# A gated cross-attention kernel: the second x load ahead of the setup's last store, both bias DMAs at later slots

## The chip, the cores and the metric

The kernel runs on one core of one Trainium2 chip. The metric is the device time of one execution in microseconds (us); the median of several runs is compared. PE is the engine for matmuls, DVE the vector engine, ACT the engine for activations and copies, POOL the general-purpose engine, SP the engine that only issues DMAs. Each engine runs its own instructions strictly in the order of the program; engines wait for each other through semaphores.

## The reference

Everything is float32. `x` is 8 x 1024 x 1024, the context (memory) 8 x 64 x 512.

```
memory_proj = einsum('bme,de->bmd', memory, W_mem)
scores  = einsum('bnd,bmd->bnm', x, memory_proj) / sqrt(1024)
attn    = softmax(scores)
context = einsum('bnm,bmd->bnd', attn, memory_proj)
gate    = sigmoid(concat([x, context]) @ W_gate.T + b_gate)
fused   = x + gate * context
out     = fused * rsqrt(mean(fused**2) + 1e-6) * norm_w
```

## The kernel before

The tokens are worked in 16 "quads" of 512 tokens, numbered from 0. The product of a quad's x with the upper half of `W_gate` is done by a fast matrix scheme with seven outer products, visited in the order 1, 6, 7, 5, 4, 2, 3; each outer product is again seven inner products (`af`, `kB`, `kC`, `ed`, `ed`, `af`, `af`), each one "slot" of the plan, so that a quad has 49 slots. For outer product o of quad q there is a set of left sums `l` (tile `l2_q_o`, four instructions on POOL, made while the outer product before it runs), two PSUM banks `af` and `ed`, and two single banks `b` (for `kB`) and `c` (for `kC`). DVE empties `kB` and `kC` into `u`, so the next outer product's `kB` on PE waits until DVE has read the last one. POOL (`pre`) adds the sums `u3` (512 wide) and `u4` (256 wide) into the tiles `gate_0` to `gate_3`, and DVE (`fin_ed`, `fin_af`) adds the banks `ed` and `af` on top; so one outer product's additions wait for POOL's, and POOL's for DVE's `u`. Below, `u_6`, `l_5`, `kB_5` and so on carry the number of the outer product.

Beside this run the attention's scores and softmax. The context's part of the gate is not computed from the context: a matrix `mg`, memory times the lower half of `W_gate`, is made once in the setup, stored to DRAM (`mgd`), and loaded for each batch element: 64 rows for each of two halves. A matmul of the attention with `mg` ("visit", `pc<-mg,attnT` and `af<-mg,attnT`) adds the gate's context part. The first visits of a quad stand in outer product 4 and use the banks `b` and `c` that its `kB` and `kC` have just used; the second stand in outer product 3.

The bias `b_gate` is added to `mg` once: a DMA that accumulates, issued by POOL, adds it to the 64 loaded rows of the first batch element in SBUF (`add_bias` on `mgs[0][M:P]`), a second, larger one (448 rows) to the rows of the other seven in DRAM (`mgd[1, M:]`). These are the first two DMAs that POOL issues; later it issues `residual`, four each quad, which add x to the gated result.

A quad's x is loaded by four DMAs of 512 KB on SP's queue (`load_xq`) into one tile `xq`; the pool has one buffer, so a load waits until the eight transposes of the quad before (DVE, `a<-xq`) have read it. The setup ends with four stores of `mg` (c11, c22, c21, c12 in this order) and `load_mg`, which waits for them.

What runs when is set by two means: the setup is written out by hand, and the main part by the table `plan(q)`, whose `at(slot, ...)` puts a call at a slot. Within an engine the program's order is kept. Slot 0 begins with the `af` matmul at 78.72 us of the profiled execution.

Of the kernel before, what the change touches and what calls it, by code (L numbers as in the profile page):

```python
# [15 lines left out]
P = 128  # L16
# [4 lines left out]
def tile_gated_cross_attention_rmsnorm(  # L21
# [44 lines left out]
    M, E = mem.shape[1:]  # L66
# [10 lines left out]
    Q4 = D // 4  # L77
# [4 lines left out]
    xqpool = ctx.enter_context(tc.tile_pool(name="xqpool", bufs=1))  # L82
# [12 lines left out]
    def tt(eng, o, a, b, op):  # L95
        pin(eng.tensor_tensor(o, a, b, op))  # L96

    def load(o, i):
        pin(nc.sync.dma_start(o, i))

    def t4k(pool, shape, tag, name):
        return pool.tile(shape, F32, tag=tag, name=name)
# [5 lines left out]
    def chunks(t, n):  # L108

        return t.rearrange("p s e -> p (s e)").rearrange("p (m j) -> p j m", j=n)  # L110
# [34 lines left out]
    load(nw_sb, norm_w.partition_broadcast(P))  # L145
    xq = {}

    def load_xq(q, i):
        b, n0 = q // QPB, (q % QPB) * QT
        if i == 0:  # L150
            xq[q] = t4k(xqpool, [P, 16, Q4], "xq", f"xq{q}")
        src = x[b, n0 : n0 + QT, :].rearrange("(s c) (i e) -> i c s e", c=32, i=4)
        load(xq[q][32 * i : 32 * (i + 1), :, :], src[i])

    R11, R21, R12, R22, T4, T1, T2 = range(7)
    outer_b = {
# [26 lines left out]
    mgd = dram.tile([2, BM, D], F32, name="mgd")  # L183
# [168 lines left out]
    sTs, attnTs, scs, mxs, dens, mps, mgs = {}, {}, {}, {}, {}, {}, {}  # L352
# [3 lines left out]
    def transpose_x(q, t, half):  # L356

        key = q, t // 2, half
        if key not in A:
            A[key] = t4k(  # L360
                apool, [P, KH, 2 * P], f"a{t // 2 + 1}{half + 1}", f"a{t // 2 + 1}{half + 1}_{q}"
            )
        r = t % 2
        pin(
            nc.vector.transpose(  # L365
                A[key][:, :, r * P : (r + 1) * P],
                chunks(xq[q][:, 4 * t : 4 * t + 4, :], KD)[:, half * KH : (half + 1) * KH],
            )
        )

    def outer_s(q, n):
        a11, a12, a21, a22 = (A.get((q, r, h)) for r in range(2) for h in range(2))
        if n == 3:
            S[q, 3] = a21
            tt(nc.vector, a21, a11, a21, ALU.subtract)
            return
        s = S[q, n] = t4k(apool, [P, KH, 2 * P], f"s{n}", f"s{n}_{q}")
        if n == 1:
            tt(nc.vector, s, a21, a22, ALU.add)
        elif n == 2:  # L380
            tt(nc.vector, s, S[q, 1], a11, ALU.subtract)
        else:
            tt(nc.vector, s, a12, S[q, 2], ALU.subtract)
# [153 lines left out]
    def store_mpT(r, h):  # L537
        load(mpd[:, h * KH : (h + 1) * KH, r * HM : (r + 1) * HM], mpT[r][h])
# [90 lines left out]
    def mg_tile(pool, tag, name):  # L629
        return t4k(pool, [P, 2, H], tag, name)  # L630
# [10 lines left out]

    s1 = mp_step(nc.vector, "s1", apool, m21, m22, ALU.add)
    store_mpT(0, 1)
    for i in range(4):
        load_xq(0, i)
    c11 = mg_tile(rot, "u", "mg_c11")
    c12 = mg_tile(rot, "u", "mg_c12")
    c21 = mg_tile(rot, "l2", "mg_c21")
# [49 lines left out]
    store_mg(c21, 1, 0)  # L698
    for t in (2, 3):
        transpose_x(0, t, 1)  # L700
    outer_s(0, 1)
    for n in range(2):
        inner_sum(nc.vector, 4, n)
# [10 lines left out]
    def at(slot, fn, *args):  # L714
        due.setdefault(slot, []).append(lambda: fn(*args))

    def mid(key, fn, *args):
        beside.setdefault(key, []).append(lambda: fn(*args))
# [5 lines left out]
    def plan(q):  # L724
        t0 = SLOTS * q
        nxt = q + 1 < NQ
        if q == 0:
            at(t0 + 7, scores, q)
            at(t0 + 8, add_scores, q)
        at(t0 + (3 if q else 8), outer_s, q, 3)  # L730
        for i, o in enumerate(ORDER):
            for part, t in ((0, 1), (1, 2)):
                if i + 1 < len(ORDER):
                    at(t0 + 7 * i + t, inner_s, q, ORDER[i + 1], part)
                elif nxt:
                    at(t0 + 7 * i + t, inner_s, q + 1, ORDER[0], part)
        at(t0 + (11 if q else 18), outer_s, q, 4)
        when = (9, 10, 11, 15, 16, 19, 23) if q == 0 else (1, 8, 9, 13, 15, 19, 23)
        steps = (
            turn_scores,  # L740
            softmax_max,
            softmax_exp,
            softmax_sum,
            softmax_scale,
            turn_attn,
            attn_difference,
        )
        for t, fn in zip(when, steps):
            at(t0 + t, fn, q)
        if not nxt:  # L750
            at(t0 + 12, load_last)
            return
        for i in range(4):
            at(t0 + 2 + (0 if q else 4 * i), load_xq, q + 1, i)
        for i, t, half in (
            (20, 0, 0), (21, 1, 0), (23, 2, 0), (25, 3, 0), (37, 2, 1), (38, 3, 1), (42, 0, 1)
        ):
            at(t0 + i, transpose_x, q + 1, t, half)
        mid((q, 3, 1), transpose_x, q + 1, 1, 1)
        mid((q, 3), scores, q + 1)  # L760
        at(t0 + 46, add_scores, q + 1)
        mid((q, 3), outer_s, q + 1, 1)
        mid((q, 3), outer_s, q + 1, 2)
        if (q + 1) % QPB == 0:
            at(t0 + 10, load_mp, (q + 1) // QPB)
            at(t0 + 29, turn_mp, (q + 1) // QPB)
            at(t0 + 31, store_mp, (q + 1) // QPB)
            at(t0 + 49, load_mg, (q + 1) // QPB)
        if q == 0:
            at(t0 + 10, add_bias, mgs[0][M:P, :])  # L770
            at(t0 + 20, add_bias, mgd[1, M:, :])

    for o in (2, 3):
        w1_place(o)
# [389 lines left out]
    for q in range(NQ):  # L1164
        plan(q)
        for o in ORDER:
            outer_product(q, o)
# [29 lines left out]
```

## Time and profile before

| what | us |
|---|---|
| median of 3 runs (lowest, highest) | 947.88 (947.78, 948.89) |
| the profiled execution's own time | 947.87 |
| its span, first to last instruction | 946.1 |
| PE busy in the span | 932.3 |
| DVE, POOL, ACT busy | 801.0, 738.8, 432.6 |
| quad 0's x issued by SP from | 32.69 |
| last store of `mg` issued | 79.53 |
| `mg` loads issued from | 80.12 |
| quad 1's x issued from | 83.06 |
| first bias DMA on POOL | 97.44 |
| second bias DMA on POOL | 106.23 |

The time of an execution is the span and 1.8 us around it. A PE that is busy for 932.3 of 946.1 us leaves little; whatever can be won or lost is in the places where PE waits. The waits are read in the view of waits by engine, then followed in the chain of waits (each step is what released the next) and in the timelines of single engines.

### The profile page before, as it was taken

Reading aid. Unit: us, or ns where it says so; the run is one execution under the profiler, and the core shown is the slowest. Engines: PE = TensorE matmul, PEld = TensorE weight load, DVE = VectorE, ACT = ScalarE, POOL = GpSimd, SP = SyncE. Lnnn points to the kernel's source line nnn. Section 1 sums busy time; section 2 is a strip of 40 time slices with the busy share of each in tenths; the row PEclk is TensorE's granted clock in tenths of the full one; section 3 lists DMA queues with packets and bytes.
Section 4 is the critical chain, followed back from the end, with each engine's and each line's share of the span. In section 5 each row is a group of like instructions: output and inputs, shape, how many; then the busy total and the mean of one; then the engine's idle time right before and its main releaser. Section 6 shows DMA issues by size and latency. Waiting matters only on the chain.

```text
span 946.1 us, 15921 instructions
## 1 busy us (share of the span) xinstructions
PE 932.3 (99%) x5572; PEld 727.5 (77%) x5572; DVE 801.0 (85%) x1267; ACT 432.6 (46%) x1111; POOL 738.8 (78%) x814
## 2 busy tenths in 40 slices
PE   9999899999999999999999999999999999999995
PEld 8646678687877778687777778787777778787774
DVE  6798788888897889888897889888897889888887
ACT  4212327263643627264543627264543617264556
POOL 5998878778696868778696868878696868868695
PEclk9999999999999999999999999999999999999998
DMA  9926565491918366491918466491918466390632
GB/s 378 309 69 149 87 113 131 106 197 36 219 58 173 95 142 138 101 200 33 216 65 168 100 136 143 96 206 28 220 65 163 106 130 150 87 205 34 135 154 90
DMA packets 71184, 128.44 MB, mean 136 GB/s; under 512 B 12608, under 2 KB 49472, under 8 KB 70848
## 3 DMA queue, kind: packets, MB, share of 16 engines
q1 hardware_dynamic: 61920, 93.86, 38.0%
q0 software_dynamic: 9184, 33.56, 19.6%
q8 instruction: 45, 0.74, 0.3%
q14 instruction: 35, 0.29, 0.1%
HBM read 87.56 MB, written 41.68 MB: 137 GB/s over the span
## 4 chain that ended last, share of the span: by engine, by line
PE 93%; DVE 2%; POOL 2%; issue 1%; DMA 1%; ACT 0%; SPq 0%; POOLq 0%; DVEq 0%; ACTq 0%
PE af L93 31%; PE ed L93 20%; PE kB L93 10%; PE pc L93 10%; PE kC L93 10%; PE psT_af L93 5%; PE pm_ctx L93 3%; PE pm_af L93 2%; PE pm_ed L93 2%; POOL gate L96 1%; DVE gate L96 1%; POOL l L96 1%; DMA wm<-in_w_mem_t 1%; PE psT_ed L93 0%; DVE u L96 0%
## 5 line engine op out<-in xcount | busy, mean ns | idle before, releaser
L96 POOL TENSOR_TENSOR gate<-gate,u 128x512 f32<-128x512 f32 (+1 forms) x224 | 245.5, 1108 | 151.7 <-DVE u L96 150.8
L795 ACT ACTIVATE gate<-gate 128x512 f32<-128x512 f32 x127 | 80.0, 631 | 182.4 <-DVE gate L96 180.8
L365 DVE STREAM_TRANSPOSE a<-xq 128x512 f32<-128x512 f32 x128 | 141.8, 1111 | 9.0 <-PE af L93 8.0
L96 POOL TENSOR_TENSOR l<-a 128x256 f32<-128x256 f32 x128 | 110.0, 859 | 17.4 <-PE af L93 15.8
L93 PE MATMUL pc<-mg,attnT 64*64 64x512 f32 x512 | 117.0, 596 | 0.1
L93 PE MATMUL kB<-it,l 128*128 128x256 f32 x448 | 115.0, 379 | 1.3 <-POOL l L96 1.3
L93 PE MATMUL ed<-it,l 128*128 128x256 f32 x448 | 115.0, 379 | 0.0
L824 DVE SCALAR_TENSOR_TENSOR gate<-gate,ss,nw_sb 128x512 f32<-128x512 f32 x120 | 110.2, 918 | 1.1
L93 PE MATMUL af<-w,a 128*128 128x256 f32 x384 | 98.5, 379 | 0.0
L1049 ACT COPY u<-af 128x256 f32<-128x256 f32 x112 | 41.5, 371 | 122.8 <-PE af L93 112.7
L96 DVE TENSOR_TENSOR gate<-gate,pc 128x512 f32<-128x512 f32 x128 | 85.5, 677 | 11.9 <-ACT gate L795 11.9
L93 PEld LDWEIGHTS kB<-it,l 128*128 128x128 f32 x448 | 85.0, 190 | 13.2 <-POOL l L96 1.6
L93 PEld LDWEIGHTS ed<-it,l 128*128 128x128 f32 x448 | 85.1, 190 | 11.6
L96 DVE TENSOR_TENSOR gate<-gate,ed 128x512 f32<-128x512 f32 x112 | 76.4, 682 | 17.3 <-POOL gate L96 15.4
L96 DVE TENSOR_TENSOR gate<-gate,af 128x512 f32<-128x512 f32 (+1 forms) x128 | 76.1, 605 | 16.3 <-PE af L93 10.5
L96 POOL TENSOR_TENSOR l<-s 128x256 f32<-128x256 f32 x96 | 84.7, 882 | 1.2 <-issue 1.2
L93 PEld LDWEIGHTS af<-w,a 128*128 128x128 f32 x384 | 73.0, 190 | 10.3 <-issue 0.5
L93 PEld LDWEIGHTS pc<-mg,attnT 64*64 64x64 f32 x512 | 32.8, 132 | 49.8 <-issue 23.3
L93 PE MATMUL ed<-it,a 128*128 128x256 f32 x256 | 67.4, 386 | 0.0
L93 PE MATMUL af<-mg,attnT 64*64 64x512 f32 (+1 forms) x380 | 67.0, 457 | 0.0
L96 DVE TENSOR_TENSOR u<-u,kB 128x256 f32<-128x256 f32 x112 | 46.0, 411 | 24.7 <-PE kB L93 23.7
L93 PE MATMUL af<-t,s 128*128 128x256 f32 x256 | 65.8, 379 | 0.0
(213 smaller groups left out, 2130.9 us busy)
## 6 DMA issues: line engine op xcount, KB each, us to landing
xq<-in_x SPq DMA_DIRECT2D x64, 512.0 KB, 10.3
gate<-in_x POOLq DMA_DIRECT2D x60, 512.0 KB, 8.3
out<-gate SPq DMA_DIRECT2D x60, 512.0 KB, 3.1
w<-in_w_gate_t SPq DMA_DIRECT2D x8, 512.0 KB, 10.2
w<-in_w_gate_t SPq DMA_DIRECT2D x2, 2048.0 KB, 16.9
mg<-mgd SPq DMA_DIRECT2D x16, 256.0 KB, 4.8
wm<-in_w_mem_t SPq DMA_DIRECT2D x4, 512.0 KB, 5.9
mpd<-mpT SPq DMA_DIRECT2D x4, 512.0 KB, 9.6
```

What stands on the lines that cost most here:

```text
L93: pin(nc.tensor.matmul(o, lhsT, rhs, start=start, stop=stop, skip_group_check=True))
L96: pin(eng.tensor_tensor(o, a, b, op))
L365: nc.vector.transpose(A[key][:, :, r * P : (r + 1) * P], chunks(xq[q][:, 4 * t : 4 * t + 4, :], KD)[:, half * KH : (half + 1) * KH],)
L795: pin(nc.scalar.activation(g, g, AF.Sigmoid))
L824: nc.vector.scalar_tensor_tensor(g[:, cols], g[:, cols], rstd[:, t % 2 : t % 2 + 1], nw_sb[:, cols], ALU.mult, ALU.mult,)
L1049: pin(nc.scalar.copy(p1, af[:, 0]))
```

## The change

Quad 1's x is no longer loaded from the table in slots 2, 6, 10 and 14, but in the setup, behind the last transpose of quad 0's x and in front of the store of c12. The first bias DMA moves from slot 10 to slot 18, the second from slot 20 to slot 24. `load_xq` issues its four parts in one call; for the other quads nothing else changes. No instruction is added or removed.

```diff
-    def load_xq(q, i):
+    def load_xq(q):
         b, n0 = q // QPB, (q % QPB) * QT
-        if i == 0:
-            xq[q] = t4k(xqpool, [P, 16, Q4], "xq", f"xq{q}")
+        xq[q] = t4k(xqpool, [P, 16, Q4], "xq", f"xq{q}")
         src = x[b, n0 : n0 + QT, :].rearrange("(s c) (i e) -> i c s e", c=32, i=4)
-        load(xq[q][32 * i : 32 * (i + 1), :, :], src[i])
+        for i in range(4):
+            load(xq[q][32 * i : 32 * (i + 1), :, :], src[i])
...
     for t in (2, 3):
         transpose_x(0, t, 1)
+    load_xq(1)
     outer_s(0, 1)
...
-        for i in range(4):
-            at(t0 + 2 + (0 if q else 4 * i), load_xq, q + 1, i)
+        if q:
+            at(t0 + 2, load_xq, q + 1)
...
         if q == 0:
-            at(t0 + 10, add_bias, mgs[0][M:P, :])
-            at(t0 + 20, add_bias, mgd[1, M:, :])
+            at(t0 + 18, add_bias, mgs[0][M:P, :])
+            at(t0 + 24, add_bias, mgd[1, M:, :])
```

PE, DVE and ACT keep their order, instruction for instruction. Two queues change.

On SP, at the end of the setup, the piece of the difference (`mg_c` are the four parts of `mg`, `mg_c_302` is c12; `xq_444` and `xq_481` are quad 1's x, `xq_928` quad 2's):

```order
 L99 DMA mgd<-mg_c_304 128x2x512
 L99 DMA mgd<-mg_c_303 128x2x512
+L99 DMA xq_444<-in_x 32x16x256 x4
 L99 DMA mgd<-mg_c_302 128x2x512
-L99 DMA mg_461<-mgd 64x1024 x2
-L99 DMA xq_481<-in_x 32x16x256 x4
+L99 DMA mg_466<-mgd 64x1024 x2
 L99 DMA xq_928<-in_x 32x16x256 x4
```

The four loads of x now stand ahead of one store and of both loads of `mg`, where they stood behind all three.

On POOL, in outer products 6 to 5 of quad 0, before (the name of a tile is followed by the outer product or, for `gate`, by the token tile):

```order
L96 TENSOR_TENSOR gate_1_496<-gate_1_496,u_6_510 128x512
L530 DMA mg_461<-in_b_gate 64x1024
L96 TENSOR_TENSOR gate_0_505<-gate_0_505,u_6_510 128x256
L96 TENSOR_TENSOR l_0_5_613<-s_0_444 128x256
L96 TENSOR_TENSOR l_0_5_613<-l_0_5_613,s_0_444 128x256
L96 TENSOR_TENSOR l_0_5_613<-s_0_444 128x256
L96 TENSOR_TENSOR l_0_5_613<-s_0_444,l_0_5_613 128x256
L96 TENSOR_TENSOR gate_3_636<-gate_1_496,u_7_606 128x512
L96 TENSOR_TENSOR gate_2_645<-gate_0_505,u_7_606 128x256
L530 DMA mgd<-in_b_gate 448x1024
L96 TENSOR_TENSOR l_0_4_668<-a_0_441 128x256
```

and the same stretch now:

```order
L96 TENSOR_TENSOR gate_1_499<-gate_1_499,u_6_512 128x512
L96 TENSOR_TENSOR gate_0_507<-gate_0_507,u_6_512 128x256
L96 TENSOR_TENSOR l_0_5_612<-s_0_449 128x256
L96 TENSOR_TENSOR l_0_5_612<-l_0_5_612,s_0_449 128x256
L96 TENSOR_TENSOR l_0_5_612<-s_0_449 128x256
L96 TENSOR_TENSOR l_0_5_612<-s_0_449,l_0_5_612 128x256
L96 TENSOR_TENSOR gate_3_635<-gate_1_499,u_7_606 128x512
L530 DMA mg_466<-in_b_gate 64x1024
L96 TENSOR_TENSOR gate_2_645<-gate_0_507,u_7_606 128x256
L96 TENSOR_TENSOR l_0_4_667<-a_0_441 128x256
```

The first bias DMA stood between the two additions of `u_6`; now it stands between the two additions of `u_7`, six instructions later. The second is gone from in front of `l_4`. It comes back a little later on POOL, between the additions of `u_5`:

```order
L96 TENSOR_TENSOR attnT_648<-attnT_648 64x256 x2
L96 TENSOR_TENSOR gate_3_635<-gate_3_635,u_5_662 128x512
L96 TENSOR_TENSOR gate_1_499<-gate_1_499,u_5_662 128x512
L530 DMA mgd<-in_b_gate 448x1024
L96 TENSOR_TENSOR gate_2_645<-gate_2_645,u_5_662 128x256
L96 TENSOR_TENSOR gate_0_507<-gate_0_507,u_5_662 128x256
```

Before, the same rows followed each other without the DMA.

More of the change, by code (lines that the diff above doesn't have):

```diff
@@ L643, in tile_gated_cross_attention_rmsnorm @@
     store_mpT(0, 1)
-    for i in range(4):
-        load_xq(0, i)
+    load_xq(0)
     c11 = mg_tile(rot, "u", "mg_c11")
@@ L752, in plan @@
             return
-        for i in range(4):
-            at(t0 + 2 + (0 if q else 4 * i), load_xq, q + 1, i)
+        if q:
+            at(t0 + 2, load_xq, q + 1)
         for i, t, half in (
```

## The prediction

> **What bounds the kernel now.** I read the page's first block, then the waits of PE, then the chain of waits around the two waits found there, then the timelines of PE, ACT, POOL and DVE between 94 and 130 us.
>
> ```profile
> PE 932.3 (99%) x5572; PEld 727.5 (77%) x5572; DVE 801.0 (85%) x1267; ACT 432.6 (46%) x1111; POOL 738.8 (78%) x814
> ```
>
> The waits of PE from 85 to 230 us (total, times, longest):
>
> ```profile
> PE af L93 <- ACT u L1049: 1.3, 1, 1.3
> PE kB L93 <- POOL l L96: 1.3, 1, 1.3
> ```
>
> PE is the bound nearly everywhere; these two waits, both in quad 0, are all the time that the change could win there. PE's timeline (start, length, what, idle before) has the places, and the pair of rows on which the argument will end:
>
> ```profile
> 102.95 1.10 PE L93 MATMUL kB<-it,l 128*128 128x256 f32 x4 [1.26 <-POOL l L96]
> ...
> 107.94 1.10 PE L93 MATMUL af<-t,l 128*128 128x256 f32 x4 [1.30 <-ACT u L1049]
> ...
> 126.71 1.03 PE L93 MATMUL kB<-it,l 128*128 128x256 f32 x4
> 127.57 1.03 PE L93 MATMUL kC<-w,l 128*128 128x256 f32 x4
> 128.53 0.65 PE L93 MATMUL pc<-mg,attnT 64*64 64x512 f32 x2
> ```
>
> The two waits are those of `kB_5` and `af_5`. Idle time is 1.26 + 1.30 = 2.56 us; the first product behind a wait also takes longer (1.10 for 1.03, at both), so some 2.7 us are at stake. The chain of waits (start, length, what) shows the cause:
>
> ```profile
> 94.82 2.62 issue
> 97.44 1.01 POOL mg L530
> 98.45 0.77 POOL gate L96
> ...
> 99.24 0.69 DVE gate L96
> ...
> 102.42 0.39 DVE u L96
> ...
> 102.91 0.43 DVE u L96
> ...
> 103.41 2.19 POOL gate L96
> ...
> 106.59 1.06 DVE a L365
> 107.66 0.63 DVE gate L96 x2
> ...
> 111.86 0.75 DVE u L96 x2
> 112.60 0.04 issue
> 112.65 0.65 PE pc L93 x2
> ```
>
> POOL stands 2.62 us ahead of its first DMA, the bias into `mg`, and spends 1.01 on it. "issue" means that nothing which the profile shows was awaited; the second bias DMA, below, has no such pause. I take it for a start-up that the first DMA of POOL pays, wherever it stands. Behind it comes `gate_0<-u_6`, and DVE cannot go on before 99.24. From there DVE is late: its read of `kB_7` at 102.42 frees bank `b`, and `kB_5` follows at 102.95. (The profile names POOL's `l_5`, which ended last; it is made in time for this product's first half, and the bank is what was free late. Either way the bias DMA stands ahead.) ACT has the other wait:
>
> ```profile
> 102.54 1.80 ACT L493 ACTIVATE sc<-sc,den 128x32 f32<-128x32 f32 x8 [5.75 <-DVE den L488]
> ...
> 107.44 0.36 ACT L1049 COPY u<-af 128x256 f32<-128x256 f32 x1
> ```
>
> ACT waits 5.75 us for a softmax sum that DVE makes late, and the copy of `u_5`, which `af_5` needs, queues behind. One cause, two waits.
>
> **The first bias DMA.** It goes from in front of `gate_0<-u_6` to in front of `gate_2<-u_7`. What it takes out of POOL's queue at the old place is 2.62 + 1.01 = 3.63 us. DVE's row at 99.24 moves to 95.61, the two `u` rows of outer product 7 to 98.79 and 99.28, and POOL's `gate_3<-u_7`, which waits for the second of them, from 103.41 to 99.78; it ends at 101.97. `kB_5` and `af_5` then have what they need in time: both waits of PE go. But now POOL meets its first DMA: 101.97 + 2.62 + 1.01 = 105.60, and `gate_2<-u_7` (0.77, as the addition behind the same DMA before) ends at 106.37. Before, it ended here:
>
> ```profile
> 103.41 2.87 POOL L96 TENSOR_TENSOR gate<-gate,u 128x512 f32<-128x512 f32 x2 [0.48 <-DVE u L96]
> 106.23 1.02 POOL L530 DMA_DIRECT2D mgd<-in_b_gate  x1
> 106.92 1.07 POOL L96 TENSOR_TENSOR l<-a 128x256 f32<-128x256 f32 x1
> ...
> 111.87 4.80 POOL L96 TENSOR_TENSOR gate<-gate,u 128x512 f32<-128x512 f32 x4
> ...
> 119.50 1.96 POOL L96 TENSOR_TENSOR gate<-gate,u 128x512 f32<-128x512 f32 x2
> ...
> 125.81 2.07 POOL L96 TENSOR_TENSOR gate<-gate,u 128x512 f32<-128x512 f32 x2 [1.49 <-DVE u L96]
> ```
>
> 103.41 + 2.87 is 106.28. So the lead of 3.63 us is given back in full: from `gate_2<-u_7` on, POOL is where it was (0.09 late, which is the rounding of 0.77 against 0.72 for such an addition).
>
> **The second bias DMA.** 1.02 us leave the place ahead of `l_4` and come back behind two of the four additions of `u_5`. `l_4` comes 1.0 earlier, and the rows at 111.87 start at 110.9; with the DMA among them they end at 111.87 - 1.0 + 4.80 + 1.0 = 116.67, as before. Between 103.41 and 125.81 POOL has no idle time in these rows: a continuous queue in which the same work changes places ends when it did. So the additions of `u_4` at 119.50 stay.
>
> **Who waits for POOL there.** DVE's rows:
>
> ```profile
> 113.64 1.76 DVE L96 TENSOR_TENSOR it<-w,it 128x512 f32<-128x512 f32 x1
> 116.02 0.69 DVE L96 TENSOR_TENSOR gate<-gate,af 128x512 f32<-128x512 f32 x1 [0.62 <-POOL gate L96]
> ...
> 120.81 0.69 DVE L96 TENSOR_TENSOR gate<-gate,ed 128x512 f32<-128x512 f32 x1 [0.78 <-POOL gate L96]
> 122.19 0.69 DVE L96 TENSOR_TENSOR gate<-gate,pc 128x512 f32<-128x512 f32 x1 [0.69 <-ACT gate L795]
> ...
> 128.01 0.39 DVE L96 TENSOR_TENSOR u<-u,kB 128x256 f32<-128x256 f32 x1
> ```
>
> At 116.02 and 120.81 DVE waits for POOL's additions of `u_5` and `u_4`. From 122.19 to 128.40 its timeline has no idle row; the last, `u<-kB_3`, frees bank `b` for `pc` at 128.53. PE will arrive there early. Its first stop comes sooner, at the first visit (112.65): DVE's second `gate_2` addition stood in the row 107.66 and can now start at 106.39 instead of 107.9 or so, and the `u` rows behind it follow 1.5 earlier, so PE is 1.5 us ahead there, not 2.7. At the second visit it must wait for 128.40. The pause from the end of DVE's row to `pc` is 0.04 at the first visit (112.60); with that, `pc` goes at 128.44 instead of 128.53. That 0.09 is the whole gain: behind it PE has no wait before or after, and the stretch that follows is unchanged.
>
> **The loads of x.** They start when the transposes of quad 0's x are done, at 72.06 + 2.12 = 74.2 (first row below), 9 us sooner, and cost PE, DVE and POOL no instruction. Quad 1's transposes begin at 106.59 in the chain, 9 us after x has landed (97.1, below), so nothing is won directly. SP's four issues are over well ahead of the c12 store at 79.53. What may be late is `mg`, behind 2 MB of x on the same queue:
>
> ```profile
> 72.06 2.12 DVE L365 STREAM_TRANSPOSE a<-xq 128x512 f32<-128x512 f32 x2 [0.99 <-PE pm_ctx L93]
> ...
> L99 SPq DMA_DIRECT2D xq<-in_x x4: 487/488/578, 83.1 to 84.7; - x4
> DMA to landing us min/median/max: 5.6/9.5/12.4
> ...
> DMA to landing us min/median/max: 3.4/3.6/3.7
> ```
>
> After DVE's last transposes of quad 0 come the landings of quad 1's x and, in the last line, of the two `mg` loads. x took from 83.1 to 84.7 + 12.4 = 97.1, that is 14.0 us; from 74.2 it ends at 88.2. If store and load go wholly behind, with 3.7 each: 88.2 + 3.7 + 3.7 = 95.6. The bias DMA asks for `mg` at 101.97. Cost nothing; the cover is 6 us.
>
> The second bias DMA, 16.4 us from issue to landing, now runs from some 114.0 to 130.4 and so into the `residual` DMAs of 127.8, the squares of which start on ACT at 141.19:
>
> ```profile
> DMA to landing us min/median/max: 16.4/16.4/16.4
> ...
> DMA to landing us min/median/max: 5.5/7.1/8.8
> ...
> 141.19 1.04 ACT L809 ACTIVATE junk<-gate 128x1024 f32<-128x1024 f32 x1
> ```
>
> Wholly behind it they land at 130.4 + 8.8 = 139.2. Cost nothing, cover 2 us.
>
> **The sum.** The profiled execution took 947.87, the median 947.88, so one stands for the other: 947.87 - 0.09 = 947.8. The uncertain term is POOL's time from 94.82 to 119.50. DVE's row at 113.64 takes 1.76, and the four additions beside it 4.80 where twice the pair at 119.50 is 3.92: this collision, worth 0.88, may go or grow by as much. That is 946.9 to 948.7. The start-up is bounded below by 0 (the second bias DMA) and above by twice 2.62; I take 2.62, from the one row there is.
>
> **Rivals.** First, the start-up does not come back: POOL's DMA code is there in time, or the pause was the place's own (x was landing then, and is not at 102). Then POOL runs 2.6 us ahead to 119.50, DVE with it, PE keeps nearly all its 2.7: 945.2. For it: one single row, no cause visible; against: nothing else shown was awaited. Half a start-up gives 946.5. Chance of less than 0.7 us of start-up, 0.17.
>
> Second, slower: the start-up is longer at its new place. Each us more is one more on POOL's queue, on DVE at 120.81 and on `pc`. Twice 2.62 gives 947.8 + 2.6 = 950.4; slower by over 0.2% from 4.6 us on. Only the one row speaks on it, and the DMA engines are idle at 102, which speaks against. 0.04. The Trainium skill, "GPSIMD Engine Reference", section "Instruction dispatch", says that the first call of a freshly loaded kernel pays about 6 us which no instruction of the profile shows; by that figure, an estimate, the time would be 947.8 + 3.3 = 951.1. This trace agrees that such a pause is hidden, and has 2.62.
>
> Third, `mg` is late: from a landing after 101.97 on, each us costs one. With the longest landing of the x loads (12.4) for store and load both, it lands at 88.2 + 24.8 = 113.0, and the kernel takes 947.8 + 11 = 959; over 0.2% from 104 on. Against it, 95.6 above. 0.03.
>
> **Chances.** What measures as no change is within 0.2%, 1.9 us. The forecast with its collisions has 0.70, a partial start-up (946.0 to 946.9) 0.06, both "same": 0.76. Faster 0.17, slower 0.07. The range reaches into the first rival to 945.3 and up to 948.8.
>
> **What would show it.** Right: "issue" of about 2.6 us on POOL's chain ahead of `mg` near 102, not at 94.8; `kB_5` 1.3 us sooner than 102.95, without idle time; PE waits instead for DVE's `u` from 107 to 111 and about 1.4 us ahead of the visit near 128.4; DVE still waits for POOL ahead of its row near 120.8; x issued at 74. Wrong: no "issue" there, and `pc` of the second visit near 126.

## The result and the profile after

The changed kernel takes 945.65 us (median of 9 runs, 945.22 to 946.12); the kernel before, beside it on the same chip, 948.47 (9 runs, 947.78 to 948.93). The ratio is 0.9972, 95% interval 0.9961 to 0.9982: faster by 0.28%. The two profiled spans are 946.1 and 943.5, a difference of 2.6 us. That is inside the range of the prediction, which was stretched down to 945.3 for its first rival, and outside its likeliest case, no measurable change: the first rival's time came true.

The page of the changed kernel, engines' busy time:

```profile
PE 932.2 (99%) x5572; PEld 727.7 (77%) x5572; DVE 803.7 (85%) x1267; ACT 432.6 (46%) x1111; POOL 738.1 (78%) x814
```

PE does the same work in the same time (932.3 before); what went is idle time. The waits of PE between 85 and 230 us:

```profile
PE pc L93 <- DVE u L96: 0.3, 1, 0.3
```

Both waits of 1.3 us are gone, and a single one of 0.3 has come. PE's timeline has the places (start, length, what, idle before): `kB_5`, `af_5`, the first visit, the second visit:

```profile
101.69 1.03 PE L93 MATMUL kB<-it,l 128*128 128x256 f32 x4
...
105.14 1.03 PE L93 MATMUL af<-t,l 128*128 128x256 f32 x4
...
109.55 0.65 PE L93 MATMUL pc<-mg,attnT 64*64 64x512 f32 x2
...
125.94 0.65 PE L93 MATMUL pc<-mg,attnT 64*64 64x512 f32 x2 [0.33 <-DVE u L96]
```

The last row stood at 128.53 before. 128.53 - 125.94 = 2.59, which is the whole difference of the spans. The reason is on POOL, whose timeline reads now:

```profile
93.70 1.96 POOL L96 TENSOR_TENSOR gate<-gate,u 128x512 f32<-128x512 f32 x2
...
99.87 2.18 POOL L96 TENSOR_TENSOR gate<-gate,u 128x512 f32<-128x512 f32 x1 [0.48 <-DVE u L96]
102.00 1.00 POOL L530 DMA_DIRECT2D mg<-in_b_gate  x1
102.76 1.00 POOL L96 TENSOR_TENSOR gate<-gate,u 128x256 f32<-128x256 f32 x1
...
108.33 2.50 POOL L96 TENSOR_TENSOR gate<-gate,u 128x512 f32<-128x512 f32 x2
110.78 1.02 POOL L530 DMA_DIRECT2D mgd<-in_b_gate  x1
```

Ahead of the DMA at 102.00, POOL's first, there is no pause at all, and none near 95 either. The 2.62 us that POOL stood there are not paid later; they are gone. DVE and ACT follow:

```profile
95.70 0.69 DVE L96 TENSOR_TENSOR gate<-gate,af 128x512 f32<-128x512 f32 x1
...
111.30 3.16 DVE L96 TENSOR_TENSOR it<-w,it 128x512 f32<-128x512 f32 x1
114.39 0.67 DVE L96 TENSOR_TENSOR gate<-gate,af 128x512 f32<-128x512 f32 x1
...
125.47 0.41 DVE L96 TENSOR_TENSOR u<-u,kB 128x256 f32<-128x256 f32 x1
```

```profile
99.00 1.80 ACT L493 ACTIVATE sc<-sc,den 128x32 f32<-128x32 f32 x8 [2.04 <-DVE den L488]
...
103.90 0.36 ACT L1049 COPY u<-af 128x256 f32<-128x256 f32 x1
```

ACT's wait for `den` fell from 5.75 to 2.04, and the copy of `u_5` comes at 103.90 (107.44 before), in time for `af_5`. SP's DMAs at line 99 from 74 us on, with the times from issue to landing:

```profile
L99 SPq DMA_DIRECT2D xq<-in_x x4: 334/483/541, 74.4 to 75.9; - x4
L99 SPq DMA_DIRECT2D mg<-mgd x2: 445/464/482, 80.2 to 89.1; - x2
L99 SPq DMA_DIRECT2D mgd<-mg_c x1: 383/383/383, 79.7 to 79.7; - x1
...
DMA to landing us min/median/max: 3.4/9.4/12.2
```

x landed at 88.07, the store of c12 at 89.06 (9.4 after its issue), the second load of `mg` at 92.44, far ahead of the 102.00 at which the bias DMA wants it.

### The profile page after: what moved, and what is told of

The parts are those of the page before. It is cut to its first block, busy times and chain, and to the rows that moved or that the text cites. A ratio compares the mean times of both kernels' runs of the same rounds, so it can differ in the third digit from the quotient of the medians.

```text
span 943.5 us, 15920 instructions
## 1 busy us (share of the span) xinstructions
PE 932.2 (99%) x5572; PEld 727.7 (77%) x5572; DVE 803.7 (85%) x1267; ACT 432.6 (46%) x1111; POOL 738.1 (78%) x814
## 4 chain that ended last, share of the span: by engine, by line
PE 94%; DVE 3%; POOL 1%; issue 1%; DMA 1%; ACT 0%; SPq 0%; POOLq 0%; DVEq 0%; ACTq 0%
PE af L93 31%; PE ed L93 20%; PE kC L93 10%; PE kB L93 10%; PE pc L93 9%; PE psT_af L93 5%; PE pm_ctx L93 3%; PE pm_af L93 2%; PE pm_ed L93 2%; DVE gate L96 1%; POOL gate L96 1%; DMA wm<-in_w_mem_t 1%; PE psT_ed L93 0%; DVE u L96 0%; PE mg_u L93 0%
## 5 line engine op out<-in xcount | busy, mean ns | idle before, releaser
L96 POOL TENSOR_TENSOR l<-a 128x256 f32<-128x256 f32 x128 | 112.6, 880 | 17.3 <-PE af L93 15.8
```

## Experiments

Where did the start-up go? Two theories at first. A: the pause is a start-up of POOL's first DMA itself. B: it is a fetch of POOL's instructions, held up by x, which in the kernel before was in transfer from 83.1 to 97.1; the DMA only happened to stand there. All kernels below are the one before with the edit shown, except the first, which is the changed one. Ratios are against the kernel before on the same chip (median 948.49 in the first four, 948.54 in the next four, 948.62 in the last four).

**x early only.** The changed kernel with the bias DMAs back at their old slots.

```diff
-            at(t0 + 18, add_bias, mgs[0][M:P, :])
-            at(t0 + 24, add_bias, mgd[1, M:, :])
+            at(t0 + 10, add_bias, mgs[0][M:P, :])
+            at(t0 + 20, add_bias, mgd[1, M:, :])
```

> Only the x loads are moved; both bias DMAs keep their old slots 10 and 20. Theory A (the pause of 2.6 us belongs to POOL's first DMA at its old place and is hidden or absent at the new one): the pause stays at about 94.8, PE keeps its two waits of 1.3, time 947.5 to 948.9 like before. Theory B (POOL waits for its own next instructions, whose fetch is held up by quad 1's x in transfer): no pause, the bias DMA costs its 1.0 us alone, PE's two waits go or fall below 0.3, time 945.3 to 946.3 like after.

Measured: 945.5, ratio 0.9969 (0.9957 to 0.998). POOL's first DMA at its old place, without x around it:

```profile
93.86 1.27 POOL L96 TENSOR_TENSOR gate<-gate,u 128x512 f32<-128x512 f32 x1
95.08 0.98 POOL L530 DMA_DIRECT2D mg<-in_b_gate  x1
```

No pause. A start-up that POOL's first DMA always pays (A) fails here.

**Bias late only.** The other half: x at its old place, the two DMAs at slots 18 and 24.

```diff
-            at(t0 + 10, add_bias, mgs[0][M:P, :])
-            at(t0 + 20, add_bias, mgd[1, M:, :])
+            at(t0 + 18, add_bias, mgs[0][M:P, :])
+            at(t0 + 24, add_bias, mgd[1, M:, :])
```

> Only the bias DMAs are moved (slots 18 and 24); x is loaded where it was, in transfer from 83 to 97. Theory A: no pause of POOL at 95, time 945.3 to 946.3. Theory B: POOL still pauses 1.5 to 3 us near 95, now ahead of an instruction that is no DMA (an addition of u_6 or a sum of l_5), DVE is late behind it, PE keeps waits of 1 to 2.6 us in all, time 947.0 to 948.9.

Measured: 945.47, ratio 0.997 (0.9959 to 0.9982). Either half alone has the whole gain; the two are not added.

```profile
100.01 2.18 POOL L96 TENSOR_TENSOR gate<-gate,u 128x512 f32<-128x512 f32 x1 [0.47 <-DVE u L96]
102.15 1.00 POOL L530 DMA_DIRECT2D mg<-in_b_gate  x1
```

And near 95, with x in transfer, POOL's other instructions run through: the additions of `u_6` start at 93.87 and 95.09, back to back. So a fetch held up by x does not by itself stop POOL (against B); here it would have had to.

**An earlier first DMA.** A small DMA of POOL into a scratch tile at 1.5 us, so that the bias is no longer its first.

```diff
+    first = small.tile([P // 2, 64], F32, tag="first", name="first")
+    pin(nc.gpsimd.memset(first, 0.0))
+    pin(
+        nc.gpsimd.dma_start(
+            first, b_gate[0:64].partition_broadcast(P // 2), accum_op=ALU.add
+        )
+    )
```

> The kernel before with one small extra DMA of POOL (64 x 64, adds part of the bias into a scratch tile that nothing reads) at the start of the setup, where POOL waits for the weights anyway. If the pause is a start-up of POOL's first DMA (theory A in its simplest form), it goes into the setup, 94.8 to 97.4 is free of it, time 945.3 to 946.3. Theory B: the pause stays near 95, two or three instructions earlier at most, time 947.5 to 948.9.

Measured: 946.39, ratio 0.9979 (0.997 to 0.9988). That is 0.9 above x early only; 0.60 of it is a wait of PE in the setup, for ACT's `pm_it`, which the kernel before does not have. Whether the new DMA causes it is not shown.

```profile
94.86 1.27 POOL L96 TENSOR_TENSOR gate<-gate,u 128x512 f32<-128x512 f32 x1
96.07 0.81 POOL L537 DMA_DIRECT2D mg<-in_b_gate  x1
```

No pause at the second DMA of POOL, at the old place and beside x. Being POOL's first DMA matters after all, and x alone does not do it.

**24 small instructions more on POOL**, in the setup, far ahead of the place.

```diff
+    pad = small.tile([P, 1], F32, tag="pad", name="pad")
+    for _ in range(24):
+        pin(nc.gpsimd.memset(pad, 0.0))
```

> The kernel before with 24 tiny memsets of a scratch tile on POOL at the start of the setup, so that every later instruction of POOL stands 24 places further on in its instruction stream; all else is as before. Theory A: pause of 2.6 ahead of the first bias DMA as before, time 947.5 to 948.9. Theory B: POOL reaches the border of its instruction block 24 instructions earlier, near 72 to 80 us and before x is in transfer, so there is no pause of more than 0.5 us, PE's waits go, time 945.3 to 946.3.

Measured: 945.49, ratio 0.9971 (0.996 to 0.9982).

```profile
94.84 0.98 POOL L533 DMA_DIRECT2D mg<-in_b_gate  x1
```

This is the first DMA, at its old place, beside x, and yet without a pause. A has no place for this, nor for x. What 24 instructions move is the point at which POOL needs the next part of its program. The trace records such fetches as packets of a queue called instruction. The view of DMA queues in the kernel before, from 83.1 to 95.1 us and from 95.1 to 96 (packets, MB, share):

```profile
q1 hardware_dynamic: 2103, 2.28, 104.0%
q8 instruction: 1, 0.02, 0.7%
...
q1 hardware_dynamic: 74, 0.06, 42.3%
q14 instruction: 2, 0.02, 9.3%
```

In this kernel no packet of queue 14 is served while x fills queue 1; at 95.21 and 95.22 come two, inside the pause of 94.82 to 97.44. (Queue 8 carries 16 KB packets, 45 in the span, and one of them was served in the time of x; by its number it could be PE's, which with PEld has by far the most instructions. Queue 14 carries 8 KB packets.) With 24 instructions more on POOL, one packet comes at 40.62 instead, and only one is left in the nineties (95.69):

```profile
q1 hardware_dynamic: 580, 0.58, 113.4%
q14 instruction: 1, 0.01, 1.3%
```

(that is the window from 39 to 42 us; the expectation had the fetch at 72 to 80). So one of the two packets was POOL's. The same window shows that a full queue 1, here with quad 0's x, does not hold such a packet back in every case. It remained to see what the pause hangs on. The next four runs put three theories against each other: POOL's first DMA waits for a held-up fetch of POOL (F); a start-up is paid at certain places only (S); the part of POOL's program that it held ended at that instruction by chance (G).

**First bias DMA at slot 4**, which is near 89 us, in the time of x.

```diff
-            at(t0 + 10, add_bias, mgs[0][M:P, :])
+            at(t0 + 4, add_bias, mgs[0][M:P, :])
```

> The kernel before with the first bias DMA at slot 4 (near 89 us; mg has landed at 86), as POOL's first DMA, while quad 1's x is in transfer until 97. Theory F (POOL's first DMA has to wait for an instruction fetch of POOL, and that fetch is held up while x is in transfer): POOL stands from about 89 until 95 to 97.5, 6 to 8 us, l_7 is late, PE waits 3 us or more, time 950 to 955. Theory S (a start-up of 2.6 us that only shows at certain places): a pause of 2.6 at 89 or none, time 945.3 to 948.9. Theory G (POOL lacks the instructions behind a border of its stream that lay at the DMA by chance): no pause at 89, a pause of 1 to 3 near 95 ahead of an addition of u_6 or a sum, time 946 to 948.9.

Measured: 945.04, ratio 0.9965 (0.9952 to 0.9978), and no pause:

```profile
87.52 1.72 POOL L96 TENSOR_TENSOR it<-t,it 128x512 f32<-128x512 f32 x1
89.18 1.00 POOL L530 DMA_DIRECT2D mg<-in_b_gate  x1
```

F as put, that the first DMA waits anywhere in the time of x, fails.

**Slot 4, with the earlier first DMA.** Both edits together.

> As the bias at slot 4, with the small extra DMA of POOL (64 x 64 into a scratch tile that nothing reads) in the setup, so that the bias DMA is POOL's second. Theory F: no pause at 89, the DMA costs its 1.0, time 945.3 to 947. Theory S: the same. Theory G: as in the run without the extra DMA, a pause near 95.

Measured: 945.61, ratio 0.9972 (0.9961 to 0.9982). With no pause to take away, this run tells nothing of the pause; the DMA stood at 90.05. PE has a wait of 0.79 for POOL in the setup, where POOL itself waits for a load; the profile of one instruction more (below) has the same wait, of 0.94, so it need not come from the extra DMA. The run has an exception, though: one packet of queue 14 came at 90.97, amid the transfer of x (84.1 to 99.7), the other at 96.95. So x does not hold every such packet to its end. Whose the early one was, and what let it through, the trace does not say.

**Slot 4, with 24 instructions more.**

> As the bias at slot 4, with 24 tiny memsets on POOL in the setup. The bias DMA is POOL's first and x is in transfer, but POOL's instruction fetch is made long before. Theory F: no pause at 89, time 945.3 to 946.5. Theory S: as without the memsets. Theory G: no pause, 945.3 to 946.5.

Measured: 944.76, ratio 0.9963 (0.9948 to 0.9978); no pause here either.

**One instruction more**, at the old place: the edit of the 24 with `range(1)`.

> The kernel before with a single tiny memset on POOL in the setup. Theory F: POOL's fetch is asked for one instruction earlier in the program, still about when x starts, so the pause of about 2.6 stays ahead of the first bias DMA, time 947.5 to 948.9 (945.3 to 946.3 without a pause if the fetch now comes ahead of x). Theory G: the pause moves to another instruction or is gone. Theory S: the pause stays.

Measured: 948.47, ratio 1.0001 (0.9992 to 1.001). The profiled execution took 949.45, with the 0.94 of waiting in the setup, so its times stand about 1 us later. The pause is back, ahead of the same instruction:

```profile
94.55 1.27 POOL L96 TENSOR_TENSOR gate<-gate,u 128x512 f32<-128x512 f32 x1
98.98 1.01 POOL L533 DMA_DIRECT2D mg<-in_b_gate  x1 [3.16 <-issue]
```

One instruction more did not shift it to the instruction ahead, which weakens G. The packets of queue 14 came at 96.79 and 96.81 here, 1.6 later than before, and the DMA started 1.5 later. That suggested theory H, which is F with a time at which the fetch is asked for: POOL's first DMA waits only if it is met while a fetch of POOL's program is out; other instructions do not wait. It is sharp on the places: the fetch must be asked for after 89.2 (slot 4 pays nothing) and ahead of 94.8, where the pause of the kernel before begins. In the run with x early only, where POOL has the same program and nothing is in the way, packets came at 90.03 and 92.80. The last four runs bracket it.

**First bias DMA at slot 7.** POOL's order is that of slot 4: the DMA stands right behind `it`, ahead of `l_7`. So this run repeats that one.

```diff
-            at(t0 + 10, add_bias, mgs[0][M:P, :])
+            at(t0 + 7, add_bias, mgs[0][M:P, :])
```

> The kernel before, with the first bias DMA at slot 7: on POOL in front of the four additions of l_7, near 90.5 us; x stays at its old place, in transfer from 83 to 97. In the kernel before, the instruction packets of POOL that were asked for during this transfer came only at 95.2, and the pause of POOL ended 1.5 us behind them (97.44; in the kernel with one more POOL instruction 96.8 and 98.98). Theory H: POOL's first DMA, when it is met while such a fetch is still out, waits until it has landed. If the fetch is asked for before 90.5: a pause of 6 to 7 us ahead of the DMA, its start near 97.4, l_7 and with it kB_7 late, 951 or more. If it is asked for later: no pause, 945. Theory G (POOL has run out of instructions at that count of instructions, whichever stands there): the DMA at 90.5 without a pause, and the pause of 2 to 3 us stays near 95, now ahead of one of the additions of u_6; 948.

Measured: 944.82, ratio 0.996 (0.9945 to 0.9975). The expectation put the DMA at 90.5; POOL reached it sooner:

```profile
89.17 1.00 POOL L530 DMA_DIRECT2D mg<-in_b_gate  x1
91.17 0.72 POOL L96 TENSOR_TENSOR l<-a 128x256 f32<-128x256 f32 x1 [1.00 <-DVE u L96]
```

No pause there, and none near 95, where G wanted one (the additions of `u_6` start at 94.03 and 95.25, back to back).

**First bias DMA at slot 8**, two additions of `l_7` later, at 92.3.

```diff
-            at(t0 + 10, add_bias, mgs[0][M:P, :])
+            at(t0 + 8, add_bias, mgs[0][M:P, :])
```

> As the run with slot 7, with the first bias DMA at slot 8: between the second and the third addition of l_7, near 92.2 us. H: a pause of about 5 us, start near 97.4, 950 to 951, if the fetch is asked for before 92.2; none and 945 if later. G: no pause at the DMA, 2 to 3 us ahead of one of the additions of u_6 near 95; 948.

Measured: 951.14, ratio 1.0027 (1.0016 to 1.0038): slower, as H had it and G had not.

```profile
91.57 0.73 POOL L96 TENSOR_TENSOR l<-l,a 128x256 f32<-128x256 f32 x1
97.85 1.01 POOL L530 DMA_DIRECT2D mg<-in_b_gate  x1 [5.55 <-issue]
98.61 1.00 POOL L96 TENSOR_TENSOR l<-a 128x256 f32<-128x256 f32 x1
```

The pause is 5.55 us, twice that of the kernel before, and it ends again as the transfer of x does, 0.78 behind x's last landing (0.32 in the kernel before). DVE did not hold POOL up in it: it has no row between 93.59 and 101.54 here. With this run the fetch must be asked for between 89.2 and 92.3. The instruction packets, from 83.3 to 95.6 and from 95.6 to 96.4:

```profile
q1 hardware_dynamic: 2162, 2.34, 101.7%
q8 instruction: 1, 0.02, 0.7%
...
q1 hardware_dynamic: 25, 0.02, 12.5%
q14 instruction: 2, 0.02, 9.5%
```

**Six instructions more**, at the old place (`range(6)`).

> The kernel before, with six small memsets on POOL in the setup. They shift POOL's own stream by six instructions, so that its fetch is asked for six instructions earlier in the program. With one instruction the pause stayed, with 24 it went, and one packet was served at 40.6 instead of in the nineties. H: if the fetch is now asked for before x is in transfer (before 83 us), no pause and 945.3; otherwise the pause of 2.6 to 3.2 us ahead of the first bias DMA stays, 948.5. G: the pause moves to an instruction six places earlier (one of l_7, near 91), or goes.

Measured: 945.37, ratio 0.9966 (0.9953 to 0.9979). The fetch came just before x's traffic, seen in the window from 83.8 to 84.6, and the DMA has no pause:

```profile
q14 instruction: 1, 0.01, 3.6%
```

```profile
94.33 1.26 POOL L96 TENSOR_TENSOR gate<-gate,u 128x512 f32<-128x512 f32 x1
95.54 0.98 POOL L533 DMA_DIRECT2D mg<-in_b_gate  x1
```

**Twelve instructions more** (`range(12)`).

> The kernel before, with twelve small memsets on POOL in the setup. H: the fetch is asked for twelve instructions earlier, which is near 77 to 83 us, mostly ahead of x: no pause, 945.3. G: the pause moves to an instruction twelve places earlier (near 82 to 85) if x holds the fetch there, or goes.

Measured: 945.58, ratio 0.9966 (0.9953 to 0.9979). The packet came at 62.85, sooner than the 77 to 83 of the expectation, the DMA at 94.84 without a pause.

The runs side by side (the packets read one by one from the trace; where two come together it can't be told which is POOL's; times in us):

| kernel | x in transfer | POOL's first DMA | packets of queue 14, 60 to 98 | pause |
|---|---|---|---|---|
| before | 83.1 to 97.1 | 97.44 | 95.21, 95.22 | 2.62 |
| one instruction more | 84.1 to 98.2 | 98.98 | 96.79, 96.81 | 3.16 |
| slot 8 | 83.2 to 97.1 | 97.85 | 95.70, 95.73 | 5.55 |
| slot 7 | 83.2 to 98.3 | 89.17 | 95.59, 96.78 | none |
| slot 4 | 83.5 to 99.3 | 89.18 | 96.56, 97.25 | none |
| slot 4, earlier first DMA | 84.1 to 99.7 | 1.51 | 90.97, 96.95 | none |
| slot 4, 24 more | 83.7 to 99.2 | 89.42 | 96.59 (and 41.99) | none |
| bias late only | 83.4 to 97.6 | 102.15 | 95.76, 95.78 | none |
| earlier first DMA | 84.0 to 98.1 | 1.51 | 96.51, 96.65 | none |
| six more | 83.9 to 97.9 | 95.54 | 83.98, 96.21 | none |
| twelve more | 83.1 to 97.2 | 94.84 | 62.85, 95.66 | none |
| 24 more | 83.2 to 97.3 | 94.84 | 95.69 (and 40.62) | none |
| x early only | 74.5 to 88.6 | 95.08 | 90.03, 92.80 | none |
| after | 74.4 to 88.1 | 102.00 | 89.89, 91.91 | none |

More instructions on POOL bring its packet forward step by step: 95.2 with none, 83.98 with six, 62.85 with twelve, 40.62 with 24. The other packet stays between 95.2 and 96.2 in these. In the three kernels with a pause, the last packet ends at 95.91, 97.44 and 96.34 (it takes 0.6 to 0.7), and the DMA starts at 97.44, 98.98 and 97.85: 1.53, 1.54 and 1.51 behind it, though the pauses are of 2.62, 3.16 and 5.55. So the runs show when the pause comes and when it ends: POOL's first DMA, met while queue 14's packets come late beside x, starts 1.5 us after they end; take away x, the packets' lateness, or the DMA's being first, and the pause is gone. That the late packet is POOL's own is inferred from the runs with more instructions. What the remaining 1.5 us are, why a DMA that isn't POOL's first does not wait (one run, the earlier first DMA), and why a packet now and then comes in the middle of such a load (40.62, 41.99, 90.97), stays open.

## Why the prediction was right in range and wrong in its likeliest case

**What held.** One cause stood behind both waits of PE: with the pause and the DMA out of POOL's queue, DVE's row came at 95.70 (predicted 95.61), `gate_3<-u_7` at 99.87 (99.78), the first bias DMA at 102.00 (101.97), `kB_5` at 101.69 without idle time. On the bank the prediction was not borne out: the view of waits had named POOL's `l_5`, whose last row ended at 102.93 in the kernel before, later than DVE's read of the bank (102.81) and 0.02 ahead of `kB_5`. `l_5` too stood behind the bias DMA and now ends at 99.39, so both go by the same change and no run separates them. The loads of x cost nothing: landed at 88.07 (88.2), `mg` at 92.44 where 95.6 was the bound, so the third rival had no ground. The second bias DMA landed at 126.91 and did not hold up `residual`.

**What failed.** The step is in "The first bias DMA": "But now POOL meets its first DMA: 101.97 + 2.62 + 1.01 = 105.60". The term of 2.62, taken again at the new place, measured 0. The premise is the sentence in "What bounds the kernel now": "I take it for a start-up that the first DMA of POOL pays, wherever it stands." The lead of 3.63 was therefore not given back; from there on the prediction's rows are late by the pause: second visit at 125.94 where 128.44 was expected, second bias DMA at 110.78 where 114.0 was. PE was 112.65 - 109.55 = 3.10 us ahead at the first visit, where 1.5 was expected. The sign shown to look for ("`pc` of the second visit near 126") came. Two readings beside it were off and cost nothing: 0.77 against 0.72 leaves 0.05 to round, not 0.09; and POOL's queue was without idle time to 124.3, not to 125.81, whose row shows 1.49 of it.

**The first rival** had the price, and part of the mechanism: "the pause was the place's own (x was landing then, and is not at 102)", PE keeping nearly all of 2.7 us; the spans give 2.6. That x was gone is enough (x early only); but it is not needed, for with x in its old place the DMA at slot 18 has no pause either (bias late only). It had a chance of 0.17, against it "nothing else shown was awaited". That was a reading of the chain of waits alone. The view of DMA queues, cut to the window of the pause, showed the two instruction packets at 95.2 in the trace of before already; with them a cause that belonged to the place was no longer invisible, and the chance should have been higher.

**The second rival's rule.** The Trainium skill, "GPSIMD Engine Reference", section "Instruction dispatch", has the first call of freshly loaded code pay about 6 us. No run here shows such a fixed price at POOL's first DMA: 0 in eleven of the fourteen kernels of the table, and where there is a pause its length follows the packet. The 5.55 of slot 8 are near that figure, but they end 1.51 behind a packet as the shorter ones do. The longer pause of this rival did not come at slot 18, but there is one at slot 8, where the kernel took 951.14.

**The collision term**, up to 0.88 either way, was read from POOL's rows, and the larger change came on DVE: its `it` now takes 3.16 instead of 1.76. The run with the bias late alone has 3.16 as well, x early alone 1.76, so it comes with the second bias DMA's new place; what collides there is not shown. It cost nothing, since DVE's next row came at 114.39, 1.6 us sooner than before.

**Whether both halves are needed** was never asked. They are not: x early alone is 945.5, the bias late alone 945.47, both 945.65 (in another comparison; the ratios 0.9969, 0.997 and 0.9972 lie in each other's intervals). Each removes the same coincidence from another side. The kernels with the first bias DMA at slots 4 and 7 and x unmoved measured 0.9965 and 0.996, with 24 instructions more besides 0.9963; they have no wait of PE between 85 and 230 us, where the changed kernel has 0.3, but their intervals overlap that of the changed kernel.

## What to carry to other kernels

A pause that the chain of waits calls "issue" can have a cause elsewhere in the trace: look in its window at the DMA queues, for instruction packets that come late behind a large load, before calling it a fixed start-up. If a change moves two things that meet at one place, ask of each alone whether the meeting still happens; one part can have the whole gain, and a third edit (a few instructions more, a slot earlier) the same. In this kernel a bulk load was better kept away from the time at which POOL issues its first DMA, unless that DMA stood ahead of the fetch or another had gone before.

## What the runs showed of the hardware

Instruction packets can come late beside data: queue 14's came at 90.03 and 92.80 with x out of the way, and at 95.21 and 95.22 with x in transfer. Not all do: three came in the middle of a large load (40.62, 41.99, 90.97). The Trainium skill, "Runtime: NRT & Kernel Launch", section "Instruction fetch mechanics", says that the sequencer fetches the next page while it executes the current one and that the cost is mostly hidden. The rows agree for ordinary instructions: with the packets late until 95.8, POOL ran on without a gap in the run with the bias late. They differ at POOL's first DMA, where up to 5.55 us of it were not hidden.

In one trace a wait of PE of 3.08 us was followed by a lower clock. PE's timeline in the kernel with slot 8, at its three waits in quad 0:

```profile
99.67 1.72 PE L93 MATMUL kC<-w,l 128*128 128x256 f32 x4 [3.08 <-POOL l L96]
101.18 1.91 PE L93 MATMUL ed<-it,a 128*128 128x256 f32 x4
102.88 1.33 PE L93 MATMUL ed<-it,l 128*128 128x256 f32 x4
104.05 1.03 PE L93 MATMUL af<-w,l 128*128 128x256 f32 x4
...
110.92 1.10 PE L93 MATMUL af<-t,l 128*128 128x256 f32 x4 [0.67 <-ACT u L1049]
...
115.65 0.65 PE L93 MATMUL pc<-mg,attnT 64*64 64x512 f32 x2 [0.17 <-DVE u L96]
```

The same view by stretches of 10 us (PE, PEld, DVE, ACT, POOL busy, then the granted clock, DMA share, GB/s):

```profile
100.00:110.00 10.00, 10.00 (x40) 8.39 (x38) 7.46 (x13) 2.12 (x9) 9.45 (x11) 0.83 0.10 19
```

The clock was 0.83 there on average, and 1.00 in this stretch of the kernel before. Cut finer, it is 0.50 from 100.10 to 103.40 and 1.00 from 103.60 on. The products from `kC_7` to the next `af` took 104.05 - 99.67 = 4.38 us, where they took 98.94 - 96.35 = 2.59 before. So of the 3.0 us by which this span is longer (949.1 against 946.1), 3.08 + 0.67 + 0.17 - 2.56 = 1.36 are idle time, and 4.38 - 2.59 = 1.79 are slow products; the two add up to 3.15, which is 0.15 more than the spans differ by. Shorter waits had no such stretch behind them: after the 1.3 us of the kernel before and the 1.8 of the one with one instruction more, the first product took 1.10, the next 1.03, and the clock was 1.00.
